# A graph layer on one core: node data fetched ahead of their blocks, edge rows stored in a new order, and SyncE's queue in program order

## The chip, the cores and the metric

The kernel runs on one core of a Trainium2 chip. The time is the device time of one execution, in microseconds (us); of before there are 14 runs with a median of 16,058.38 us (16,052.2 to 16,063.84). One more execution was profiled. Engines are called TensorE (PE, and PEld for its weight loads), VectorE (DVE), ScalarE (ACT), GpSimd (POOL) and SyncE (SP); SPq and so on are their instruction queues.

## The reference, cut to what matters

A graph has 50,000 nodes with 160 features each (64 scalars s, 32 vectors v of three parts) and 1,650,000 edges, sorted by their destination; 50,000 of them lead from a node to itself. Each edge has four numbers e (e0 and e1). A message is made for each edge and summed per destination:

```python
ss, vv = s[src], v[src]
dot = einsum('eui,ei->eu', vv, e1)
out0 = C0 * (ss * e0 @ W1 + dot * INV3 @ W2)
out1 = C1 * (p3 + p4 + p5)         # from ss, vv, e0, e1 and W3, W4, W5
m_agg = segment_sum(concat(out0, out1), dst)
h = concat(m_agg_s @ Ws, m_agg_v @ Wv)
y = x + relu(h);  out = layernorm(x + y)
```

A message is linear in x[src] and in e, so sums of e_k * x[src] over the edges of a node can be formed first, and one 640 x 160 weight matrix (BW, made of all seven W) applied to them.

## The kernel before, in words

**Plain and packed groups.** Edges are taken in groups of 6 x 128 (G = 6), two groups to a pair, twenty to a step `s` of the edge list. For each 128 edges GpSimd issues one indirect gather of 128 rows of x into the tile xg (L302), 12 to a pair. VectorE makes from the destinations a one-hot matrix of 32 slots (hot, L311) and multiplies it by the four numbers of each edge (ha, L314; three buffers). TensorE sums ha x xg into ps (L324), ScalarE copies it out (A, L327). xg has five buffers of a pair each (pool `rows`). The gather needs the index tile si, the matrix ha needs rel and pk; `place` (L262 to L296) makes all of them for one step s by transposes on TensorE.

**Self edges.** An edge from a node to itself needs no gather, since a block of nodes reads its own x in order anyway. So all but the first HEAD = 60 groups are packed beforehand: `pack(c)` reads 120 rows of 790 edges, finds in each row the self edges (`count`, `mark`, `collect`: their four numbers go to the tile mine), closes the holes that they leave by five shifts of 1, 2, 4, 8, 16 places (L490 to L506, two halves each), and stores the rows one after another into a list `edges` in DRAM, and mine into `selves`. There are 17 packs. Where a row begins in the list is known only at run time, from the table that `row_table` computes (L350); SyncE loads those numbers into registers (L519, L522) and issues two DMAs for each row, one to edges and one to selves (L540). Stored rows overlap by what the packing left over at their ends; so before, first all tails (from place 32 on), then all heads (32 places) are stored, in 12 rounds of up to 10 rows each. A later step s reads r from edges (L238).

**Blocks of 128 nodes.** Two pairs make a chunk: its sums are transposed (`turn`), multiplied by the weights (`apply_weights`) and kept (hp). Once the chunks of a block are complete, `nodes` loads xt (its x) and sa (its numbers from selves), `own` computes the block's own messages (ptx, xT, yx, t), `block` gathers the chunks' sums by a product (phb), adds t, and normalizes; `do_send` stores out.

**Order.** The main loop runs over the 1,043 pairs; `after_pair(p + n, f)` puts a piece of work n pairs later. The steps of a pack are spread evenly over the pairs up to a due pair, which lies one step s ahead of the first reader of the pack's rows. From this program order a scheduler makes the order on each engine, SyncE included. Every engine then works through its own list strictly in turn. SyncE issues nearly all plain DMAs: loads, row stores, sends.

**Start.** Before the loop the first step s is placed, the row table is made and the weights are multiplied together; SyncE also stores zeros into the first part of selves (L703).

Of the kernel before, what the change touches and what calls it, by code (L numbers as in the profile page):

```python
# [48 lines left out]
P = 128  # L49
# [18 lines left out]
HEAD = 60  # L68
# [31 lines left out]
def tile_gnn_resnorm(ctx: ExitStack, tc: tile.TileContext, x, src, dst, attr, W1, W2, W3, W4, W5, Ws, Wv, out, n_edges):  # L100
# [110 lines left out]
    with tc.tile_pool(name="once", bufs=1) as once, tc.tile_pool(name="raw", bufs=2) as rawp, \  # L211
            tc.tile_pool(name="idx", bufs=2) as idxp, tc.tile_pool(name="rows", bufs=5) as rowp, \
            tc.tile_pool(name="far", bufs=3) as farp, \
            tc.tile_pool(name="ops", bufs=3) as op, tc.tile_pool(name="sums", bufs=4) as sump, \
            tc.tile_pool(name="hp", bufs=alive + 4) as hpp, tc.tile_pool(name="node", bufs=3) as np_, \
            tc.tile_pool(name="psC", bufs=1, space=PSUM) as psC, tc.tile_pool(name="psK", bufs=2, space=PSUM) as psK, \
# [10 lines left out]
        dq = nc.sync  # L227
        offsets = {}
# [20 lines left out]
        def cast(loaded):  # L249
            s, n, ri, sf, df, af = loaded  # L250
            if ri is not None:
                rf = rawp.tile([P, 2, P], F32, name="rf")
                nc.scalar.copy(rf[:n], ri[:n])
                sf, df = rf[:n, 0, :], rf[:n, 1, :]
            if HELP:

                ro = rawp.tile([P, P], I32, name="ro")
                nc.scalar.mul(ro[:n], sf, 4.0 * D)
                offsets[s] = ro
            return s, n, sf, df, af  # L260

        def place(cast_):  # L262

            s, n, sf, df, af = cast_
            ng = n // G

            first = idxp.tile([P, SG], F32, name="first")
            nc.vector.tensor_scalar(first[:n], starts[:n], df[:, 0:1], None, op0=ALU.mult)
            nc.tensor.matmul(bank[:, 3, :ng], ones[:n], first[:n, :ng], start=True, stop=True)
            gs = slice(s * SG, s * SG + ng)  # L270
            nc.vector.tensor_scalar(baseB[:, gs], bank[:, 3, :ng], float(N - 1), None, op0=ALU.min)
            for g in range(QG):
                r = slice(g * W, (g + 1) * W)
                for c0, c1, h in ((s * SG // QG, (s * SG + ng) // QG, g),
                                  ((s * SG + ng) // QG, math.ceil((s * SG + ng) / QG), min(g, ng % QG - 1))):
                    if c0 < c1:
                        nc.vector.tensor_scalar(rowid[r, c0:c1],
                                                baseB[r, c0 * QG:c1 * QG].rearrange("p (c g) -> p c g", g=QG)[:, :, h],
                                                pidx[r], float(-g * W), op0=ALU.add, op1=ALU.add)
            pi = bank[:, 1:3, :]  # L280
            nc.tensor.transpose(pi[:, 0, :n], sf, ident[:n, :n])
            nc.tensor.transpose(pi[:, 1, :n], df, ident[:n, :n])
            pk = psK.tile([P, NK, P], F32, name="pk")
            for k in range(NK):
                nc.tensor.transpose(pk[:, k, :n], af[:, :, k], ident[:n, :n])
            si = idxp.tile([P, P], I32, name="si")
            nc.vector.tensor_scalar(si[:, :n], pi[:, 0, :n], 0.0, float(N - 1), op0=ALU.max, op1=ALU.min)
            rel = idxp.tile([P, P], F32, name="rel")

            nc.vector.scalar_tensor_tensor(  # L290
                rel[:, :n].rearrange("p (g j) -> p g j", j=G), pi[:, 1, :n].rearrange("p (g j) -> p g j", j=G),
                float(N - 1), baseB[:, gs].unsqueeze(2).to_broadcast([P, ng, G]),
                op0=ALU.min, op1=ALU.subtract)
            nc.vector.tensor_reduce(extremes[:, 0, s:s + 1], rel[:, :n], axis=AX.X, op=ALU.min)
            nc.vector.tensor_reduce(extremes[:, 1, s:s + 1], rel[:, :n], axis=AX.X, op=ALU.max)
            return si, rel, pk  # L296
# [53 lines left out]
        def row_table(tmp):  # L350

            NT = npacks * RP
            ti = once.tile([1, NT], I32, name="ti")
            at = tmp.tile([1, NT], F32, name="at")
            node = tmp.tile([1, NT], F32, name="node")
            nc.vector.memset(ti, 0)
            with nc.allow_non_contiguous_dma(reason="one number of each row"):
                dq.dma_start(ti[:, :NR], dst[EH:EH + NR * L].rearrange("(o r e) -> o r e", o=1, e=L)[:, :, 0])
            nc.gpsimd.iota(at, pattern=[[L, NT]], base=0, channel_multiplier=0, allow_small_or_imprecise_dtypes=True)
            most, least = math.ceil(EH / degree) + FAR, max(math.floor(EH / degree) - FAR, 0)  # L360
            nc.vector.tensor_scalar(node, ti, float(N), float(-most), op0=ALU.min, op1=ALU.add)
# [5 lines left out]
            nc.vector.tensor_copy(moved.bitcast(I32), node)  # L367
            nc.vector.tensor_copy(node, moved.bitcast(I32))
# [3 lines left out]
            nc.vector.tensor_scalar(moved, ti, float(N), None, op0=ALU.min)  # L372
            nc.vector.tensor_tensor(moved[:, :NR], moved[:, :NR], node[:, :NR], op=ALU.subtract)
            nc.vector.tensor_reduce(strayed[0:1, 0:1], moved[:, :NR], axis=AX.X, op=ALU.min)
            nc.vector.tensor_reduce(strayed[0:1, 1:2], moved[:, :NR], axis=AX.X, op=ALU.max)
            by_round = "o (c i j) -> o c j i"
            nc.vector.tensor_scalar(ti.rearrange("o (c j i) -> o c j i", c=npacks, j=RS),
                                    at.rearrange(by_round, c=npacks, j=RS), float(4 * C), None, op0=ALU.mult)
            nodes_at = moved.bitcast(I32)
            nc.vector.tensor_scalar(nodes_at.rearrange("o (c j i) -> o c j i", c=npacks, j=RS),  # L380
                                    node.rearrange(by_round, c=npacks, j=RS), float(4 * NK), None, op0=ALU.mult)
            return ti, nodes_at

        def pack(c):
# [128 lines left out]
            def store(head, j):  # L513

                m = len(range(j, n, RS))
                if not m:
                    return
                i0 = r0 + j * (RP // RS)
                _, at = nc.values_load_multi_w_load_instructions(  # L519
                    row_at[0:1, i0:i0 + m], engines=[ET.SP], min_val=0, max_val=row_start(NR - 1)[0][1] * 4 * C,  # L520
                    skip_runtime_bounds_check_because="held within bounds")
                _, node = nc.values_load_multi_w_load_instructions(  # L522
                    node_at[0:1, i0:i0 + m], engines=[ET.SP], min_val=0, max_val=row_start(NR - 1)[1][1] * 4 * NK,
                    skip_runtime_bounds_check_because="held within bounds")
                for i in range(m):
                    p = j + i * RS
                    (lo, hi), (nlo, nhi) = row_start(r0 + p)
                    v = nc.s_assert_within(at[i], lo * 4 * C, hi * 4 * C,
                                           skip_runtime_bounds_check_because="held within bounds")
                    e = slice(0, W) if head else slice(W, L)  # L530
                    put(edge_bytes, v, e, C, T["rows"][p:p + 1, e, :])
                    if r0 + p < real:
                        v = nc.s_assert_within(node[i], nlo * 4 * NK, nhi * 4 * NK,
                                               skip_runtime_bounds_check_because="held within bounds")
                        e = slice(0, W // 2) if head else slice(W // 2, W)
                        put(self_bytes, v, e, NK, T["mine"][p:p + 1, 0, e, :])

            def put(mem, at, e, width, what):
                size = (e.stop - e.start) * width * 4
                dq.dma_start(mem[e.start * width * 4:][ds(at, size)].rearrange("(o f) -> o f", o=1),  # L540
                             what.bitcast(U8).rearrange("p e c -> p (e c)"))
# [4 lines left out]
            for head in (False, True):  # L546
                steps += [partial(store, head, j) for j in range(RS)]
# [36 lines left out]
        def nodes(b):  # L584

            nb, row = rows_of(b)
            cs = of_block[b]
            xt = np_.tile([P, D], F32, name="xt")
# [3 lines left out]
            sa = np_.tile([P, NK], F32, name="sa")  # L592
            dq.dma_start(sa[:nb], selves[0, row.start * NK:row.stop * NK].rearrange("(n k) -> n k", k=NK))
            rr = np_.tile([P, alive], F32, name="rr")
# [4 lines left out]
            return xt, sa, hot2  # L599

        def own(b, xt, sa, hot2):
# [7 lines left out]
            t = np_.tile([P, D], F32, name="t")  # L609
# [12 lines left out]
            return xt, t, hot2  # L622
# [55 lines left out]
        placed = {0: place(cast(load(0)))}  # L678

        strayed = once.tile([P, 2], F32, name="strayed")  # L680
        nc.vector.memset(strayed, 0.0)
        moved = once.tile([1, npacks * RP], F32, name="moved")
        with tc.tile_pool(name="begin", bufs=1) as beginp:
            row_at, node_at = row_table(beginp)
            weights(beginp, psM)
        packp = later_pools.enter_context(tc.tile_pool(name="pack", bufs=1))
        limit = once.tile([P, 1], F32, name="limit")
        nc.vector.memset(limit, float(KM))
        place_ = once.tile([P, L], F32, name="place")
        nc.gpsimd.iota(place_, pattern=[[1, L]], base=0, channel_multiplier=0, allow_small_or_imprecise_dtypes=True)  # L690
        nc.vector.tensor_scalar(place_, place_, degree, None, op0=ALU.add)
# [6 lines left out]
        nc.vector.memset(counts[:, 1], float(W))  # L698

        nz = math.ceil((row_start(0)[1][1] + W) / P)  # L700
        zeros = once.tile([P, nz * NK], F32, name="zeros")
        nc.vector.memset(zeros, 0.0)
        dq.dma_start(selves[0, 0:P * nz * NK].rearrange("(p f) -> p f", p=P), zeros)  # L703
# [11 lines left out]
        def do_weights(c):  # L715
            hps[c] = apply_weights(*parts.pop(c))
            for b in after[c]:
                of_nodes[b] = nodes(b)
# [22 lines left out]

        raws, has = {}, {}
# [11 lines left out]
        done, began = 0, 0  # L754
        for p, (s, g, ng) in enumerate(pairs):
# [13 lines left out]
            if packs:  # L769
# [8 lines left out]
            if (g + ng) % QG == 0 or g + ng == NG:  # L778
                after_pair(p + 1, do_turn, c, sums)
                for b in after[c]:  # L780
                    after_pair(p + 3, do_own, b)
# [3 lines left out]
                    after_pair(p + 7, do_send, b)  # L785
# [197 lines left out]
```

## Time and profile before

| what | value |
|---|---|
| median of 14 runs | 16,058.38 us |
| the profiled execution's own time | 16,067.85 us |
| its span, first to last instruction | 16,066.1 us |
| GpSimd busy | 11,854.4 us (74%), 12,516 gathers |
| TensorE busy | 12,329.0 us (77%) |
| VectorE busy | 6,412.3 us (40%) |
| ScalarE busy | 1,573.8 us (10%) |
| granted TensorE clock, mean | 0.689 |
| moved by DMA | 1,218.18 MB, 76 GB/s |
| share of the chain that ended last | GpSimd 46%, issue 21%, TensorE 15%, DMA 13%, SyncE's queue 4% |
| first gather begins, last gather ends | 24.16 us, 16,012.55 us |

In a group's line stand the source line, engine and operation, what it writes and reads, and the count; then its busy time in all and the mean of one in ns; then the idle time of the engine just ahead of such instructions, and what ended most of it. "issue" is time in which an engine waited for nothing that the profile shows. In a list of waits each line names who waited for whom, the sum in us, how many times, and the longest. A timeline gives start and duration in us, and in brackets the idle time before. A table by stage gives for each stretch the busy time and count of PE, PEld, DVE, ACT and POOL, the granted clock, the DMA share and GB/s. A source line's row gives the shortest, median and longest duration in ns.

### The profile page before, as it was taken

How to read it: one execution, taken by the hardware profiler on the slowest of the kernel's cores; microseconds unless marked ns; L12 is line 12 of the kernel's file. 1: busy time of each engine (PE TensorE's matmuls, PEld its weight loads, DVE VectorE, ACT ScalarE, POOL GpSimd, SP SyncE). 2: the span in 40 equal slices, each digit the busy share in tenths (PEclk: the TensorE clock that was granted, in tenths of full speed). 3: DMA queues.
4: the chain of work that ended last, by engine and by line, in shares of the span. 5: the costliest groups of instructions: out<-in, count | busy, mean ns of one | idle time of the engine just before them, and what ended most of it. 6: DMA issues, size and time to landing. Idle time of an engine off the chain costs nothing.

```text
span 16066.1 us, 155475 instructions
## 1 busy us (share of the span) xinstructions
PE 12329.0 (77%) x47011; PEld 8690.3 (54%) x47012; DVE 6412.3 (40%) x15105; ACT 1573.8 (10%) x3873; POOL 11854.4 (74%) x12530
## 2 busy tenths in 40 slices
PE   6186877787778777787878777787878777787887
PEld 4155555555555555555555555555555555555555
DVE  4353434343443434353444434343444434253222
ACT  0011010010101010010101010010101010010100
POOL 7277777777777777777777777777777777777776
PEclk6576666666776767676776767676776666676666
DMA  2133333323333333333333333333333332332322
GB/s 72 34 76 79 77 81 76 81 73 82 75 80 77 78 80 77 80 76 80 75 81 77 78 78 77 80 76 78 75 81 77 78 78 74 77 76 76 75 72 62
DMA packets 813417, 1218.18 MB, mean 76 GB/s; under 512 B 288531, under 2 KB 591540, under 8 KB 808506
## 3 DMA queue, kind: packets, MB, share of 16 engines
q0 software_dynamic: 600768, 1026.11, 26.0%
q1 hardware_dynamic: 211196, 181.54, 4.2%
q8 instruction: 373, 6.11, 0.2%
q14 instruction: 472, 3.87, 0.1%
q10 hardware_dynamic: 608, 0.55, 0.0%
HBM read 1135.43 MB, written 71.86 MB: 75 GB/s over the span
## 4 chain that ended last, share of the span: by engine, by line
POOL 46%; issue 21%; PE 15%; DMA 13%; SPq 4%; DVE 1%; ACT 0%; POOLq 0%; DVEq 0%; ACTq 0%
POOL xg L302 46%; DMA xg<-in_x,si 12%; PE ps L324 7%; PE yx L614 2%; PE yx L613 2%; SPq L540 2%; PE pt L559 1%; PE phb L630 1%; PE phc L573 1%; SPq L522 1%; SPq L519 1%; PE ptx L607 0%; DMA edges<-prow 0%; DVE pra L465 0%; DVE prow L504 0%
## 5 line engine op out<-in xcount | busy, mean ns | idle before, releaser
L302 POOL DMA_INDIRECT xg<-in_x,si x12516 | 11850.1, 947 | 4157.6 <-issue 3573.0
L324 PE MATMUL ps<-xg,ha 128*128 128x160 f32 x25032 | 7379.0, 423 | 3190.3 <-DMA xg<-in_x,si 3133.5
L324 PEld LDWEIGHTS ps<-xg,ha 128*128 128x128 f32 x25032 | 4964.9, 253 | 5533.8 <-DMA xg<-in_x,si 4971.9
L314 DVE TENSOR_TENSOR ha<-hot,pk 128x1536 f32<-128x1536 f32 x1043 | 1825.5, 1750 | 5380.1 <-PE ps L324 5380.1
L465 DVE SCALAR_TENSOR_TENSOR pra<-marks,prow 120x236 bf16<-120x236 f32 (+40 forms) x2924 | 1499.2, 513 | 33.0
L327 ACT COPY A<-ps 128x320 f32<-128x320 f32 x1043 | 443.4, 425 | 6525.4 <-PE ps L324 6489.5
L614 PE MATMUL yx<-BWb,xT 32*128 32x320 f32 x1564 | 988.5, 727 | 0.9 <-ACT xT L608 0.9
L613 PE MATMUL yx<-BWa,xT 128*128 128x320 f32 x1564 | 954.3, 709 | 0.7 <-ACT xT L608 0.6
L559 PE MATMUL pt<-ident,A 128*128 128x128 f32 (+1 forms) x4172 | 916.9, 371 | 43.6 <-DVE t L620 31.0
L562 ACT COPY at<-pt 128x512 f32<-128x512 f32 (+1 forms) x1044 | 600.7, 580 | 3222.3 <-PE pt L559 3202.6
L630 PE MATMUL phb<-hp,hot 128*128 128x160 f32 x4688 | 897.3, 353 | 0.0
L630 PEld LDWEIGHTS phb<-hp,hot 128*128 128x128 f32 x4688 | 854.0, 237 | 15.8 <-ACT at L562 10.4
L573 PE MATMUL phc<-BWa,at 128*128 128x160 f32 x4176 | 783.2, 339 | 1.0 <-ACT at L562 1.0
L559 PEld LDWEIGHTS pt<-ident,A 128*128 128x128 f32 (+1 forms) x4172 | 642.8, 166 | 231.2 <-issue 113.1
L573 PE MATMUL phc<-BWb,at 32*128 32x160 f32 x4176 | 766.1, 326 | 0.0
L573 PEld LDWEIGHTS phc<-BWa,at 128*128 128x128 f32 x4176 | 727.3, 225 | 7.0 <-ACT at L562 6.4
L573 PEld LDWEIGHTS phc<-BWb,at 32*128 32x128 f32 x4176 | 632.6, 199 | 104.5 <-issue 104.5
L614 PEld LDWEIGHTS yx<-BWb,xT 32*128 32x128 f32 x1564 | 347.6, 276 | 601.0 <-ACT xT L608 299.0
L618 DVE TENSOR_SCALAR t<-yx,sa 128x160 f32<-128x160 f32 x391 | 149.3, 382 | 1194.4 <-PE yx L614 1193.3
L631 DVE TENSOR_TENSOR phb<-phb,t 128x160 f32<-128x160 f32 x391 | 129.6, 331 | 1184.3 <-PE phb L630 974.7
L620 DVE SCALAR_TENSOR_TENSOR t<-yx,sa,t 128x160 f32<-128x160 f32 x1173 | 443.2, 378 | 325.5 <-PE yx L614 319.8
L311 DVE TENSOR_TENSOR hot<-bank,rel 128x384 f32<-128x384 f32 x1043 | 562.0, 544 | 3.5
(148 smaller groups left out, 4539.2 us busy)
## 6 DMA issues: line engine op xcount, KB each, us to landing
xg<-in_x,si POOLq DMA_INDIRECT x12516
selves<-mine SPq DMA_DIRECT2D x4062, 0.2 KB
r<-edges SPq DMA_DIRECT2D x101, 360.0 KB
edges<-prow SPq DMA_DIRECT2D x2033, 17.8 KB
edges<-prow SPq DMA_DIRECT2D x2033, 0.8 KB
xt<-in_x SPq DMA_DIRECT2D x390, 80.0 KB
out<-o SPq DMA_DIRECT2D x390, 80.0 KB
pra<-in_attr SPq DMA_DIRECT2D x16, 1481.2 KB
```

Of the source, the lines that this page charges most:

```text
L302: nc.gpsimd.indirect_dma_start(out=xg[:, j, :], out_offset=None, in_=x, in_offset=bass.IndirectOffsetOnAxis(ap=placed[0][:, u + j:u + j + ...
L311: nc.vector.tensor_tensor(hot[:, :n], slotsP[:, 0:W].unsqueeze(1).to_broadcast([P, n, W]), rel[:, u:u + n].unsqueeze(2).to_broadcast([P, n ...
L314: nc.vector.tensor_tensor(ha[:, :n], hot[:, :n].unsqueeze(2).to_broadcast([P, n, NK, W]), pk[:, :, u:u + n].rearrange("p k u -> p u k").un ...
L324: nc.tensor.matmul(ps[:, j // G, :], ha[:, j].rearrange("p k w -> p (k w)"), xr, start=j % G == 0, stop=j % G == G - 1)
L327: evict(A[:, :ng], ps[:, :ng])
L465: nc.vector.scalar_tensor_tensor(T["waste"][:n, w0:w1], T["marks"][:n, w0 - a:w1 - a], float(w + 1), T["rows"][:n, w0:w1, 2 + k], op0=ALU. ...
L559: nc.tensor.transpose(pt[:f1 - f0, g, :], A[:, i, f0:f1], ident)
L562: evict(at[:, :, :ng].rearrange("f k g w -> f g k w"), pt[:f1 - f0, :ng].rearrange("f g (k w) -> f g k w", w=W))
L573: nc.tensor.matmul(ph[:ng * W], at[:, k, :ng].rearrange("f g w -> f (g w)"), bw[:, k, :], start=i == 0, stop=i == 2 * NK - 1)
L613: nc.tensor.matmul(y[:nb], xT[:, 0, :nb], BWa[:, ks, :], start=True, stop=False)
L614: nc.tensor.matmul(y[:nb], xT[:D - P, 1, :nb], BWb[:, ks, :], start=False, stop=True)
L630: nc.tensor.matmul(ph[:nb], hot2[:r, i, :nb], hp[:r], start=i == 0, stop=i == len(cs) - 1)
```

## The change

- HEAD goes from 60 to 100: the first 100 groups are plain, so they also gather their self edges.
- Rows are stored whole: first the rows of even number, then the odd ones, then the heads of the even ones again. The two tables of places become one (spots), read by one load of 20 numbers for each round; with offsets that begin at zero, a DMA needs no register operation. Each of the 18 rounds is followed by three empty steps.
- xt and sa are loaded by `ahead`, 7 pairs before the block's last pair, and own messages are made 3 pairs before it (7 buffers each for xt, sa, t); before, both came 2 to 3 pairs after. The send of out moves from 7 to 8 pairs after.
- SyncE keeps the program order (`manual_schedule`), the other engines are still scheduled.
- The weights and the row table (with the zeros) move from ahead of the loop to its first two pairs, behind the first step's cast, transposes and last reduction; packs begin at pair 2.
- xg has four buffers instead of five.

In the changed program there are 12,522 gathers and 1,044 ha; SyncE has 2,991 + 2,988 row DMAs (before 4,066 + 4,062), 306 register loads (816) and 3 register operations (4,066). On VectorE the ten half shifts of a pack stand nearly together, with at most two spreads (ha) among them; before, they lay among about 12.

```diff
-HEAD = 60
+HEAD = 100
...
-            tc.tile_pool(name="idx", bufs=2) as idxp, tc.tile_pool(name="rows", bufs=5) as rowp, \
+            tc.tile_pool(name="idx", bufs=2) as idxp, tc.tile_pool(name="rows", bufs=4) as rowp, \
...
+            tc.tile_pool(name="ahead", bufs=7) as aheadp, \
...
-                i0 = r0 + j * (RP // RS)
-                _, at = nc.values_load_multi_w_load_instructions(
-                    row_at[0:1, i0:i0 + m], engines=[ET.SP], min_val=0, max_val=row_start(NR - 1)[0][1] * 4 * C,
...
-                    node_at[0:1, i0:i0 + m], engines=[ET.SP], min_val=0, max_val=row_start(NR - 1)[1][1] * 4 * NK,
+                ni = RP // RS
+                i0 = (c * RS + j) * 2 * ni
+                _, spot = nc.values_load_multi_w_load_instructions(
+                    spots[0:1, i0:i0 + 2 * ni], engines=[ET.SP], min_val=0,
...
-                    e = slice(0, W) if head else slice(W, L)
-                    put(edge_bytes, v, e, C, T["rows"][p:p + 1, e, :])
+                    put(edge_bytes, v, T["rows"][p:p + 1, :W if head else L, :])
...
-            for head in (False, True):
-                steps += [partial(store, head, j) for j in range(RS)]
+            for head, j0 in ((False, 0), (False, 1), (True, 0)):
+                for j in range(j0, RS, 2):
+                    steps += [partial(store, head, j), None, None, None]
...
+        def ahead(b):
+
+            nb, row = rows_of(b)
+            xt = aheadp.tile([P, D], F32, name="xt")
+            dq.dma_start(xt[:nb], x[row, :])
...
+            sa = aheadp.tile([P, NK], F32, name="sa")
+            dq.dma_start(sa[:nb], selves[0, row.start * NK:row.stop * NK].rearrange("(n k) -> n k", k=NK))
+            return xt, sa
...
-            t = np_.tile([P, D], F32, name="t")
+            t = aheadp.tile([P, D], F32, name="t")
...
-        with tc.tile_pool(name="begin", bufs=1) as beginp:
-            row_at, node_at = row_table(beginp)
-            weights(beginp, psM)
...
+        START = 2
+        AHEAD = 7
...
+        for at, bs in zip(complete, after):
+            for b in bs:
+                after_pair(max(at - AHEAD, START - 1), do_ahead, b)
+                after_pair(max(at - AHEAD + 4, START), do_own, b)
+        later_pools.enter_context(tc.manual_schedule(engines={ET.SP}))
...
+            if p == START - 2:
+                with ExitStack() as behind, tc.tile_pool(name="begin", bufs=1) as beginp:
+                    for i in first_ones:
+                        behind.enter_context(tc.issue_after(i))
+                    weights(beginp, psM)
+            if p == START - 1:
+                with ExitStack() as behind, tc.tile_pool(name="table", bufs=1) as tablep:
+                    for i in first_ones:
+                        behind.enter_context(tc.issue_after(i))
+                    row_table(tablep)
...
-            if packs:
+            if packs and p >= START:
...
-                    after_pair(p + 3, do_own, b)
...
-                    after_pair(p + 7, do_send, b)
+                    after_pair(p + 8, do_send, b)
```

## Prediction, made before the changed kernel was run

> **What bounds the kernel now.** I read the page first. GpSimd issues one gather for each 128 edges, and its row is the largest that nothing else hides:
>
> ```profile
> L302 POOL DMA_INDIRECT xg<-in_x,si x12516 | 11850.1, 947 | 4157.6 <-issue 3573.0
> ```
>
> Each gather takes 947 ns and 0.30 us of issue follows it, so one starts every 1.251 us; 12,515 such steps make 15,652 us (by the finer 1.2507) of a span of 16,066.1. TensorE's 77% is an average that follows this beat: in the rest of the kernel it finishes a pair's sums 2.7 us after the pair's last gather. So the time is the gathers' beat, plus whatever stops GpSimd, plus the two ends. Next I asked what GpSimd waited for, and where:
>
> ```profile
> POOL xg L302 <- issue: 3573.0, 11726, 0.3
> POOL xg L302 <- DVE si L287: 306.0, 2, 286.2
> ...
> 485.80 0.95 POOL L302 DMA_INDIRECT xg<-in_x,si  x1 [0.30 <-issue]
> 772.90 0.94 POOL L302 DMA_INDIRECT xg<-in_x,si  x1 [286.16 <-DVE si L287]
> ```
>
> One hole of 286.2 us, and 19.9 us before the first gather. The chain of waits over 440 to 780 us says what fills the hole; the table by stage says that every engine is empty in it:
>
> ```profile
> by line: SPq L540 39.0%; issue 14.8%; SPq L519 12.7%; SPq L522 12.3%; DVE prow L504 7.9%; DVE pra L465 2.0%; DVE marks L497 1.7%; DVE pri L501 1.6%; DVE pri L502 1.4%; DVE pri L499 1.4%; DMA r<-edges 1.4%; DVE ha L314 0.5%; PE ps L324 0.3%;
> ...
> 762.43 4.59 DMA r<-edges
> ```
>
> ```profile
> 500.00:600.00 100.00, 0.00 (x0) 0.00 (x0) 0.00 (x0) 0.00 (x0) 0.00 (x0) 0.50 0.04 16
> 600.00:700.00 100.00, 0.00 (x0) 0.00 (x0) 0.00 (x0) 0.00 (x0) 0.00 (x0) 0.50 0.02 7
> ```
>
> SyncE is storing the first pack of rows, 480 DMAs from 493 to 761 us, and the first packed groups (r from edges) cannot be read before the last lands. VectorE had finished packing only at 494 us, GpSimd had used up its 60 plain groups (360 gathers) at 486 us. From SyncE's own rows: 12 rounds of tails take 143.4 us (0.392 us a DMA, with a register operation in it), 12 rounds of heads 124.6 us (0.322 us a DMA); the rest of a round is two register loads:
>
> ```profile
> L519 SPq TENSOR_LOAD <-ti x408: 956/1840/2700, 496.9 to 14890.4; - x136
> ```
>
> **The change, part by part, against the profiled execution (16,067.85 us, span 16,066.1).**
>
> *100 plain groups, shorter stores.* The first packed groups are wanted at gather 600, not 360. The first gather starts near 8.5 us (below) and the first pairs lose some 12 us, so gather 600 is due at 8.5 + 12 + 600 x 1.2507 = 771 us. Is the load there? In the changed order VectorE's last shift of the first pack stands behind 33 spreads (ha), and the 33rd needs the sums of pair 29, done near 470 us. The shifts then run almost without a break: ten of about 5.2 us (0.57 + 0.56 + 0.65 + 0.59 + 2.78 by the rows of L497 to L504), the last two 3.4 us, 48 us, so stores begin near 520 us. A pack is now 18 rounds (even rows whole, odd rows whole, even heads), 20 DMAs each, no register operation: 20 x 0.322 = 6.4 us, plus one load of 20 words. Two loads of 10 cost 3.6 us on the mean; the shortest single ones 1.2 us. The Trainium skill, "Runtime: NRT & Kernel Launch", Instruction fetch mechanics, speaks against a gain here: about 200 ns for each register even in bulk, so 20 words cost 4.0 us however they are split; the row (1,840 ns for 10) says 184 ns a word. I take 3.7 us: 10.1 us a round, 182 us a pack (158 with 2.4 us, 220 if a round stays at 12.2). With about 15 us for other DMAs on the queue the load is read at 722 us, and the index si, after casts and transposes, is ready near 735: 35 us early. TensorE's transposes of r stand after 46 pairs, near 710 us, so it waits about 15 us there, within its reserve. The hole goes: -285.9 us. At 220 us a pack it would leave under 10. The 100 groups carry self edges too: 12,522 gathers instead of 12,516, 6 x 1.25 = +7.5 us.
>
> *Start.* Now the first gather starts at 24.16 us: the ti load (14 us) stands ahead of what it needs on VectorE, and the zeros store takes 10.4 us on SyncE. With both behind, the first ra lands at 5.0 us, the second, issued right behind it, near 6.8. From the transposes to the gather took 4.1 us (20.02 to 24.16), 1.2 of them another step's. I take 8.5 us (8 to 12): -15.7. But the row table now runs beside gathers, and here a rule weighs:
>
> ```profile
> 24.10 2.26 DVE L364 SCALAR_TENSOR_TENSOR node<-at,node 1x2040 f32<-1x2040 f32 x1
> 24.16 3.83 POOL L302 DMA_INDIRECT xg<-in_x,si  x1 [19.88 <-DVE si L287]
> 26.67 1.20 DVE L365 TENSOR_SCALAR node<-node 1x2040 f32<-1x2040 f32 x1
> 27.93 1.20 DVE L367 CAST moved<-node 1x2040 int32<-1x2040 f32 x1
> 28.29 2.22 POOL L302 DMA_INDIRECT xg<-in_x,si  x1 [0.30 <-issue]
> 29.19 1.20 DVE L368 CAST node<-moved 1x2040 f32<-1x2040 int32 x1
> ```
>
> The first four gathers took 3.83, 2.22, 3.20, 2.69 us, 8.1 us over their beat, and two end 0.12 us after a table step ends. The skill's "SBUF — State Buffer" (SBUF: two separate sides) says that VectorE in its two-port mode, or with two SBUF inputs against a GpSimd operation that reads SBUF, shuts GpSimd out for the whole instruction. If it is cold code that slows the first gathers, nothing changes; by the rule 15 us of table steps now fall on gathers instead of 11.7, and at 8.1 / 11.7 they cost 10.5. I take +4 (0 to +7). The iota of the table goes into GpSimd's own queue after gather 43: 1.82 + 0.3 = +2.1. The weights (a chain of small products, stores and reloads) lie under the first pairs: wanted after 3.6 pairs (about 70 us), ready near 67; a few us late would be TensorE's alone.
>
> *x and own messages ahead; SyncE in program order.* At 1302 to 1470 us the second pack's stores hold up xt:
>
> ```profile
> PE ptx L607 <- DMA xt<-in_x: 72.8, 2, 50.6
> ...
> 1491.53 0.94 POOL L302 DMA_INDIRECT xg<-in_x,si  x1 [12.83 <-PE ptx L607]
> ```
>
> TensorE stands 50 us for x, falls 88 us behind, and the gathers lose 12.5 us. xt will be asked for 7 pairs before its block is complete and transposed 3 before: 4 pairs, 60 us of cover. -12.5 us. What is added: SyncE now waits in order, so a send of out (8 pairs after its block) holds xt, sa, r and stores behind it. A block's last product stands about 5 pairs after completion, so SyncE passes a send some 3 pairs (45 us) ahead of the gathers; TensorE waits for xt and r, GpSimd for si. Stores come at most 1.2 rounds a pair (72 of 279 steps over 60 pairs), 12 us plus 1 us of other DMAs out of 15, so no backlog grows. Without this cover, each us of delay is a us. Cost 0.
>
> *Row buffers 5 to 4.* TensorE may lag 3 pairs less the usual 2.7 us, 42 us, instead of 57. Outside the two places above its lag never passed 38.2 us. But the changed order bunches the shifts of every pack: 44 to 56 us of VectorE between two spreads. Spreads run up to three pairs (45 us) ahead, so TensorE gets 8 to 20 us behind: inside 42. Cost 0; if the cover failed, the surplus is paid in each of 17 packs.
>
> *Tail.* After the last sums TensorE now runs four blocks' own messages: 6.7 + 3.6 + 4.1 + 5.8 = 20.2 us of the 53.5 after the last gather. In the changed order none is left there. What is late next is the products of the last three blocks, which stay. -20.2 us.
>
> **Sum.** -285.9 - 15.7 - 12.5 - 20.2 + 7.5 + 4 + 2.1 = -320.7: span 15,745.4, own time 15,747. The profiled run lies 9.5 us above the median of before (16,058.38), so **15,738 us**, 2.0% less. Own range 15,705 to 15,770: the start, the table and the tail by 5 to 15 us each, and 13 us that slow gathers lost at 13.54 ms, which need not return.
>
> **Rivals.**
> 1. *Bunched shifts and four buffers.* If TensorE's lag passes 42 us by 10 in each of 16 packs, +160: 15,900. For: up to 56 us in which no spread or PSUM release comes, where before they were spread over 12 pairs. Against: the sum above leaves over 20 us. Chance 0.12.
> 2. *The hole only shrinks.* Stores begin at 540 and rounds cost 13 us: r near 795, and some 60 us stay: 15,800. For: VectorE finished 110 us after its position said (384 us) in before. Against: that was one run of steps which is now mostly spread. Chance 0.10.
> 3. *SyncE in order is slower than before.* To lose the 320 us, each of 16 packs must cost 20 us of gathers beyond about 90 us of reserve (SyncE's 45 us, the row buffers' 42): 110 us of backlog over 18 rounds, 6 us a round more than the 12 us a pair allows, so from about 18 us a round on. The longest round now is 12.2. A little beyond, 16,100. Chance 0.04.
>
> The first case has 0.74. A measurement of this kernel tells 0.2% (32 us) from no change. Faster by more (below 16,026): all of cases one and two of the rivals, bar 0.02, so 0.94; within 0.02; slower 0.04. The range runs from 15,700, where everything but the beat is at its best, to 15,860, which takes in the shrunken hole and half of rival 1.
>
> **What would show it.** Right: no gap over 20 us on GpSimd; r landing before 760 us; first gather by 12 us; rounds of 9 to 11 us; 30 to 36 us after the last gather. Wrong: GpSimd waiting for ps every 60 pairs (rival 1), for si near 771 us (rival 2), or TensorE waiting for xt or r in the middle (rival 3).

## The result, and the profile after

The changed kernel takes 15,824.84 us (median of 6 runs, 15,822.25 to 15,828.87) against 16,058.38 us: 0.9855 of the time before, 95% interval 0.9845 to 0.9864, so 1.45% less where 2.0% was forecast. The profiled execution took 15,823.29 us with a span of 15,821.5 us, 244.6 us less than before. The forecast for the span was 15,745.4 us: 76 us of the expected gain are missing.

What GpSimd waited for, in the changed kernel:

```profile
POOL xg L304 <- issue: 3597.3, 11809, 0.3
POOL xg L304 <- PE ps L326: 251.7, 547, 52.0
...
529.15 0.94 POOL L304 DMA_INDIRECT xg<-in_x,si  x1 [0.30 <-issue]
530.39 0.95 POOL L304 DMA_INDIRECT xg<-in_x,si  x1 [0.30 <-issue]
583.30 0.94 POOL L304 DMA_INDIRECT xg<-in_x,si  x1 [51.96 <-PE ps L326]
```

The wait of 286 us for si is gone. In its place stands one that the prediction did not have: 52 us for a free row buffer, that is, for TensorE's sums ps. A second of 27.7 us follows after the gather at 1,214.4 us. (Nearly all the rest of the 251.7 us is in waits of the length of the usual 0.3 us of issue.) Over the beat of 1.2507 us the two holes cost 51.7 and 27.4 us, 79.1 us in all: the size of the missing gain. What did TensorE wait for, and SyncE? Between 425 and 640 us:

```profile
PE ptx L616 <- DMA xt<-in_x: 95.9, 2, 91.7
...
SPq L543 <- DVE prow L510: 262.3, 1, 262.3
...
562.99 0.38 SPq L593 DMA_DIRECT2D xt<-in_x  x1
...
565.58 0.47 PE L616 MATMUL ptx<-ident,xt 128*128 128x128 f32 x1 [91.73 <-DMA xt<-in_x]
```

```profile
480.00:520.00 40.00, 0.00 (x0) 0.00 (x0) 38.23 (x90) 0.00 (x0) 30.25 (x33) 0.50 0.27 66
520.00:560.00 40.00, 0.00 (x0) 0.00 (x0) 18.66 (x15) 0.00 (x0) 8.60 (x10) 0.50 0.11 32
560.00:600.00 40.00, 33.31 (x174) 25.97 (x175) 11.82 (x25) 5.75 (x16) 12.74 (x14) 0.79 0.19 54
```

The two waits are to be read from the bottom up. SyncE keeps program order. It came to the first row store 262 us before VectorE had made the rows (the last shift ends at 539 us), and stood there. The load of xt for the block that TensorE handles after pair 29 stands behind that store and behind 24 us of further stores: it goes out at 563 us, and TensorE begins on it 2.6 us later. So TensorE stood 91.7 us (no matmul from 480 to 560 us in the table), used up its reserve of four row buffers, and GpSimd lost what was left over. The second hole is the same thing in the second pack: SyncE stands 224 us at the first store, TensorE waits 64.6 us for xt and GpSimd 27.7 us for ps.

The other lines that answer to those shown of before: SyncE's register loads, then the row table beside the gathers.

```profile
L526 SPq TENSOR_LOAD <-spots x306: 1379/1406/1766, 275.4 to 14898.3; - x153
```

```profile
79.49 2.26 DVE L371 SCALAR_TENSOR_TENSOR node<-at,node 1x2040 f32<-1x2040 f32 x1
79.79 3.51 POOL L304 DMA_INDIRECT xg<-in_x,si  x1 [0.30 <-issue]
81.97 1.20 DVE L372 TENSOR_SCALAR node<-node 1x2040 f32<-1x2040 f32 x1
```

A load of 20 words takes 1.4 us; two loads of 10 had taken 3.6 us on the mean. A gather that meets two steps of the table takes 3.51 us instead of 0.94 and ends 0.13 us after the second of them.

### The profile page after: what moved, and what is told of

It is laid out like the page before. It is cut to its first block, busy times and chain, and to the rows that moved or that the text cites. A ratio compares the mean times of both kernels' runs of the same rounds, so it can differ in the third digit from the quotient of the medians.

```text
span 15821.5 us, 146272 instructions
## 1 busy us (share of the span) xinstructions
PE 12177.9 (77%) x47031; PEld 8563.3 (54%) x47032; DVE 6392.4 (40%) x15106; ACT 1569.9 (10%) x3876; POOL 11851.4 (75%) x12536
## 4 chain that ended last, share of the span: by engine, by line
POOL 47%; issue 21%; PE 16%; DMA 12%; DVE 4%; ACT 0%; SPq 0%; ACTq 0%; DVEq 0%; POOLq 0%
POOL xg L304 47%; DMA xg<-in_x,si 11%; PE ps L326 7%; PE yx L623 3%; PE yx L622 2%; PE pt L564 2%; DVE prow L510 1%; PE phc L578 1%; PE phb L639 1%; DMA edges<-prow 1%; PE ptx L616 0%; DVE marks L503 0%; DVE pri L507 0%; DVE ha L316 0%; DMA r<-edges 0%
## 5 line engine op out<-in xcount | busy, mean ns | idle before, releaser
L326 PE MATMUL ps<-xg,ha 128*128 128x160 f32 x25044 | 6948.3, 411 | 2831.3 <-DMA xg<-in_x,si 2675.3
L326 PEld LDWEIGHTS ps<-xg,ha 128*128 128x128 f32 x25044 | 4812.2, 247 | 4888.1 <-DMA xg<-in_x,si 4369.1
L623 PE MATMUL yx<-BWb,xT 32*128 32x320 f32 x1564 | 1042.8, 764 | 0.0
L639 PE MATMUL phb<-hp,hot 128*128 128x160 f32 x4694 | 999.4, 379 | 8.7 <-ACT at L567 8.7
L622 PE MATMUL yx<-BWa,xT 128*128 128x320 f32 x1564 | 988.2, 732 | 5.5 <-ACT xT L617 5.5
L639 PEld LDWEIGHTS phb<-hp,hot 128*128 128x128 f32 x4694 | 933.2, 256 | 49.0 <-ACT at L567 45.8
L564 PEld LDWEIGHTS pt<-ident,A 128*128 128x128 f32 (+1 forms) x4174 | 602.5, 161 | 329.1 <-issue 228.0
L578 PEld LDWEIGHTS phc<-BWa,at 128*128 128x128 f32 x4176 | 714.8, 222 | 13.6 <-ACT at L567 12.5
L617 ACT COPY xT<-ptx 128x128 f32<-128x128 f32 (+2 forms) x782 | 204.0, 261 | 4511.0 <-PE ptx L616 4428.9
```

What stands on the lines that cost most here:

```text
L326: nc.tensor.matmul(ps[:, j // G, :], ha[:, j].rearrange("p k w -> p (k w)"), xr, start=j % G == 0, stop=j % G == G - 1)
L564: nc.tensor.transpose(pt[:f1 - f0, g, :], A[:, i, f0:f1], ident)
L578: nc.tensor.matmul(ph[:ng * W], at[:, k, :ng].rearrange("f g w -> f (g w)"), bw[:, k, :], start=i == 0, stop=i == 2 * NK - 1)
L622: nc.tensor.matmul(y[:nb], xT[:, 0, :nb], BWa[:, ks, :], start=True, stop=False)
L623: nc.tensor.matmul(y[:nb], xT[:D - P, 1, :nb], BWb[:, ks, :], start=False, stop=True)
L639: nc.tensor.matmul(ph[:nb], hot2[:r, i, :nb], hp[:r], start=i == 0, stop=i == len(cs) - 1)
```

## The experiments

One thing has to be known for the numbers. Of the twelve runs only one (shifts apart) fell on a chip like that of the first runs, where the kernel before takes 16,058 us. On the four chips of the other eleven (here the late chips) it takes 21,006 to 21,089 us. Their absolute times cannot be set beside the forecast; ratios to before on the same chip, and what waits for what, can be compared among themselves. I begin with what is different there.

**The changed kernel again.** No edit.

> The changed kernel once more, beside the kernel before on this call's chip. The first four experiments ran on a chip on which the kernel before takes 21,082 us instead of 16,058, and TensorE gets its instructions late. If this call's chip is like that of the first runs: 0.985 to 0.987 of before, about 15,825 us of 16,058. If it is the late one: TensorE is the bound, the 286 us of the hole weigh less there and four row buffers and bunched shifts weigh more; I expect 0.97 to 1.01 of before.

Measured: 20,358.71 us, 0.9692 of before (0.9674 to 0.9711), just under the range that was expected. A gather still takes 946 ns, but a pair takes 19.2 to 19.7 us in most stretches of 60 pairs instead of 15.04, and GpSimd waits 3,685 us for ps instead of 252. So GpSimd now waits for TensorE all along. Matmuls of one pair on it, from the timeline:

```profile
9015.07 1.90 PE L326 MATMUL ps<-xg,ha 128*128 128x160 f32 x12
9017.28 0.57 PE L326 MATMUL ps<-xg,ha 128*128 128x160 f32 x3 [0.31 <-issue]
9019.40 0.30 PE L326 MATMUL ps<-xg,ha 128*128 128x160 f32 x1 [1.56 <-issue]
9021.50 0.42 PE L326 MATMUL ps<-xg,ha 128*128 128x160 f32 x1 [1.81 <-issue]
```

Twelve matmuls follow one another at 0.14 us, then single ones 2 us apart, although the gathers that they read had ended 53 to 62 us earlier, and the last DMA packets of these gathers 1.2 to 1.6 us after that. "issue" means that the profile shows nothing awaited: 1,515 us of it stand ahead of ps, 31 us on the first chip. That TensorE gets its instructions late is my reading, and it cannot be all: TensorE also waits 1,801 us for ScalarE's xT (85 us on the first chip), and ScalarE and GpSimd stand some 10,300 and 912 us for something that the profile does not find on this core (none on the first chip). Two plain rivals fall short: the granted clock is 0.66 there against 0.69, under 4% less, and a DMA packet of the gathers takes 111 ns on the mean, on the first chip 112. The cause stays open. The first hole's chain is the same as on the first chip, only longer:

```profile
PE ptx L616 <- DMA xt<-in_x: 121.6, 1, 121.6
...
SPq L543 <- DVE prow L510: 304.9, 1, 304.9
```

**xt off SyncE.**

```diff
-            dq.dma_start(xt[:nb], x[row, :])
+            nc.scalar.dma_start(xt[:nb], x[row, :])
...
-            dq.dma_start(sa[:nb], selves
+            nc.scalar.dma_start(sa[:nb], selves
```

> The loads of xt and sa go out on ScalarE's queue, all else as in the changed kernel (15,825 us; two holes of 51.7 and 27.4 us over the beat on GpSimd, near 530 and 1,214 us). Theory 1: the holes come from SyncE, which stands 262 us in program order at the first row store and holds xt behind it; so both go, TensorE no longer waits for xt, and the time falls by 60 to 80 us, to about 15,750. Theory 1b: behind xt stand VectorE's bunched shifts of the first pack, which hold TensorE's PSUM buffers; then only the second hole goes and half of the first: about 15,775. Theory 2: the two first packs are squeezed into 37 and 49 pairs and four row buffers do not cover it, whatever xt does; both holes stay within 10 us, about 15,825.

> xt and sa on ScalarE's queue again, hoped to be on a chip like that of the first runs. There the changed kernel has holes of 51.7 and 27.4 us. On the late chip this kernel's TensorE no longer waited for xt, but 118 us for the first step of the next place (bank from first), which stands on VectorE behind the bunched shifts. Theory 1 (SyncE's hold of xt is the whole cause): both holes go, 15,745 us. Theory 1b (behind xt stand the shifts): the second hole goes, of the first 15 to 40 us stay: 15,765 to 15,790 us. If neither hole shrinks, 15,825 us, xt was not the cause.

Measured: 1.0305 of before (1.0286 to 1.0324) and 1.0307 (1.0285 to 1.0328), 6% slower than the changed kernel on such chips. Theory 1 falls in its simple form. Between 300 and 1,200 us TensorE no longer waits for xt, but (second run; the first gives 118.4 and 65.5 us):

```profile
PE bank L271 <- DVE first L270: 118.0, 1, 118.0
...
PE pk L287 <- DMA r<-edges: 63.5, 1, 63.5
```

The hole behind pair 36 stays, 134.8 and 129.5 us long. Behind the late xt stands `first`, the first step of the next `place`, which VectorE has after the bunched shifts; behind that stands r, since the stores come late too (SyncE stands 392 us at the first). Over the whole run TensorE waits 2,192 us for r (63 times) instead of 699 us (15 times), which goes with the 6%; why r is late there so often stays open.

**SyncE scheduled.**

```diff
-        later_pools.enter_context(tc.manual_schedule(engines={ET.SP}))
```

> Only SyncE's program order is undone: its queue is arranged by the scheduler, as before the change. Theory 1 (the order holds xt, and issues a pack's four reads in one burst, which costs the gathers 1.5 to 2.5 us a pack): the holes shrink to under 20 us in all and the bursts cost less; 15,730 to 15,770 us. Rival: the program order is what keeps stores and reads early enough, and without it GpSimd waits for r or si as in the kernel before: over 15,850 us.

> SyncE scheduled, 100 groups, again. On the late chip TensorE did not wait for xt in the first packs, but 107 us for the first packed groups (r), since the scheduler set loads and sends between the stores. On a chip like that of the first runs the groups are wanted earlier in time, at 771 us: I expect a hole of 30 to 90 us near pair 46, and back the 79 us of the two others and 15 to 25 us of the bursts: 15,750 to 15,815 us. If SyncE's program order is what removed the old hole of 286 us, over 15,900 us.

Measured: 0.9128 (0.9109 to 0.9146) and 0.9126 (0.911 to 0.9142): with the program order undone the kernel is 6% faster than the changed kernel on these chips. TensorE waits in the first packs neither for xt nor for `first`, but for r, and there GpSimd's hole is now (107.7 and 105.2 us):

```profile
PE pk L287 <- DMA r<-edges: 105.1, 1, 105.1
```

Why r is late here is not what the second expectation says. One store goes out at 702 us; the other 359 begin at 789 us, when VectorE's last shift ends, and take 207 us. In the changed kernel on such a chip the 360 stores take 277 us, but begin at 681 us. So the stores are shorter and VectorE is later. The first pack's hole is as long either way (100 us in the changed kernel there), only earlier and for xt. What differs over the whole run is SyncE: it stands 8 us in all for the rows of a store (prow), against 3,765 us, and TensorE waits once for r, against 15 times (699 us). But in this kernel the ten half shifts of a pack also lie among 3 to 6 spreads instead of 0 to 2: VectorE's order, too, was made differently because SyncE's was. Which of the two gives the 6% was to be told by the next kernel but one.

**SyncE scheduled, 140 plain groups.** As the last, with

```diff
-HEAD = 100
+HEAD = 140
```

> The changed kernel with SyncE's queue arranged by the scheduler and 140 plain groups instead of 100. With SyncE scheduled alone, the hole came back as a wait of TensorE for the first packed groups (r, 107 us), while xt and the shifts of the packs no longer held it. 40 more groups are 20 pairs, 308 us of beat: r then lies in time, and no hole of over 20 us is left; 8 more gathers cost about 10 us. On a chip like that of the first runs: about 15,740 us (15,720 to 15,765), 0.980 of before, under the changed kernel by 70 us or more. On a chip where TensorE's instructions come late: about 100 us below the 19,257 us with SyncE scheduled alone, 0.906 to 0.911 of before. Rival: what holds TensorE in the first packs is the squeezed pack work on VectorE, not SyncE's order; then a hole of over 25 us stays near pair 36.

> SyncE scheduled and 140 groups, again. On the late chip it left no hole over 26 us. On a chip like that of the first runs: 15,825 less 79 (the two holes) less 15 to 25 (the bursts of reads) plus 7.5 us (6 more gathers): 15,735 us (15,720 to 15,760), the fastest of all. If a hole of over 25 us stays, above 15,770.

Measured: 0.907 (0.9055 to 0.9085) and 0.9063 (0.9046 to 0.908), as expected for such a chip by the first text. No wait of TensorE for xt, `first` or r is left between 300 and 1,200 us, and GpSimd's longest for ps is 26 us. So on these chips the first pack's hole has three layers, one behind the other: xt, `first` behind the shifts, r. Taking away one shows the next; with room for all three it is gone.

**Shifts apart.** SyncE stays in program order; each half shift is put behind the latest spread, with three empty steps after it.

```diff
+            def behind_spread(g):
+                with tc.issue_after(spreads[-1]):
+                    next(g, None)
...
-                steps += [partial(next, g, None)] * (4 if 2 << b <= KM else 2)
+                steps += [partial(behind_spread, g), None, None, None] * (4 if 2 << b <= KM else 2)
```

> The changed kernel with SyncE still in program order, but the shifts of a pack held apart: each half shift stands behind the latest spread (ha), with three empty steps after it, so they lie among 4 spreads instead of 0 or 1, and no stretch of VectorE without a spread is over about 30 us (before 44 to 56). Theory: of the 1,100 us by which SyncE's scheduled queue (19,257 us) beat the changed kernel (20,359 us, the same kind of chip, on which TensorE has no reserve), most came by VectorE's order, because the planner bunches the shifts when SyncE keeps program order; then this kernel gains 300 us or more, 0.945 to 0.955 of before. Rival: it came from SyncE's queue itself (xt, r and reads late behind stores); then within 100 us of the changed kernel, 0.965 to 0.973. On a chip like that of the first runs, where TensorE's reserve covers the bunches, both say within 15 us of 15,825 us.

Measured, on a chip like the first (before 16,057.52 us): 15,765.41 us (15,764.97 to 15,769.22), 0.9819 of before (0.9803 to 0.9836), 59 us less than the changed kernel and the fastest version measured on such a chip. I had expected under 15 us: a miss, and a useful one. The gain is in the holes: the second is gone, and the first has shrunk:

```profile
592.04 0.95 POOL L305 DMA_INDIRECT xg<-in_x,si  x1 [0.30 <-issue]
615.94 0.94 POOL L305 DMA_INDIRECT xg<-in_x,si  x1 [22.95 <-PE ps L328]
```

```profile
PE ptx L622 <- DMA xt<-in_x: 59.5, 1, 59.5
...
SPq L549 <- DVE prow L512: 218.9, 1, 218.9
```

What I had overlooked: the empty steps also move the first store later in program order. In SyncE's list 10 loads of xt stand ahead of it instead of 8. The xt that is held is that of a later block, and it is held 59.5 us instead of 91.7. The hole follows the wait: 91.7 us of waiting gave a hole of 51.7, 64.6 gave 27.4, 59.5 gave 22.7, and a wait of 22.3 us, later among this kernel's first stores, gave none. In its second pack TensorE does not wait for xt, though SyncE stands 147.3 us at the first store there: what stands behind it is not wanted yet. Each hole is the wait for xt less 37 to 40 us, which is what the four row buffers cover. Both edits act in this kernel; how much of it the shifts gave, and how much the later store, it does not tell. In the other packs SyncE now stands 82 to 109 us at the first store instead of 190 to 218, the wait of TensorE for r that the changed kernel has there (see below) is gone, and TensorE's largest lag fell from 36 to 39 us to 17 to 27 us, which cost no time here in either kernel. What the same kernel does where TensorE has no reserve was not seen, so what gives the scheduled queue its 6% there stays open.

**60 plain groups.**

```diff
-HEAD = 100
+HEAD = 60
```

> Only HEAD goes back from 100 to 60, so the first packed group is wanted at gather 360, near 470 us. If the 100 groups are what removes the hole of 286 us, it returns: shifts end near 480 us at the earliest, 18 rounds of 9.3 us take 167 us, index and transposes about 30 us more, so si is ready near 680 us and GpSimd waits about 200 us; with 6 gathers less, about 16,000 us (15,950 to 16,040). If the new order of stores and of SyncE were enough by itself, under 15,900 us.

Measured: 20,465.66 us, 0.9708 (0.969 to 0.9727), no clear difference from the changed kernel's 0.9692 (0.9674 to 0.9711). Expected was a wait for si of about 200 us; there is none over 7 us. Instead SyncE stands 369 us at the first store, TensorE waits four times for xt between 300 and 1,200 us, 288.9 us in all, and GpSimd for ps, 134.9, 49.5 and 25.1 us before gather 360 and 37.4 us ahead of it. These holes hide the rows rather than acquit them: si for the first packed groups is ready only at 766.7 us, 26 us after the last plain gather ended. Without the holes GpSimd would have been there some 200 us earlier (an estimate: their sum). So this run does not show that 60 groups are enough; it shows that at 60 groups xt is late first.

**Before, with 100 plain groups alone.** Same edit, in the other direction, on the kernel before.

> The kernel before with HEAD = 100 and nothing else of the change. If the 100 groups carry nearly all of the gain: stores begin near 540 us, the old 24 rounds take 268 us, si is ready near 825 us against gather 600 due at 787 us, so a hole of about 40 us stays of 286, and 6 gathers add 7.5 us: about 15,820 us (15,800 to 15,870), as fast as the whole change. If the shorter stores and the order of SyncE are needed as well, the hole keeps over 100 us: above 15,900 us.

> The kernel before with 100 groups alone, again. Old stores: 268 us from about 540 us, si ready near 825 us against gather 600 due near 787 us: a hole of about 40 us instead of 286, and 7.5 us for 6 gathers: 15,820 us (15,800 to 15,870), 0.983 to 0.988 of before. If shorter rounds are needed as well, over 15,900 us.

Measured: 0.9836 (0.9817 to 0.9855) and 0.986 (0.984 to 0.988). The ratio came as expected, not the way to it: a wait for si of 199 and 202 us stays, where 40 us were expected. One store goes out at 663 us, but the rest begin only at 771 us, when VectorE's last shifts end, and take 342 us for the old 24 rounds. In the changed kernel on such a chip the 18 rounds begin at 681 us and take 277 us, and there is no wait for si. So on these chips the shorter stores and an earlier start of them were needed for that hole. And in the second run TensorE waits 2,679 us for xt, 55 times, against 223 us, twice, in the changed kernel: the loads made ahead work, outside the first two packs.

**Reads spread.** Each pack's large read is cut in four, with empty steps between.

```diff
-            steps += [read, None, None, None, begin]
+            steps += [read] + [s for a in range(0, RP, 30) for s in (None, partial(read_part, a, a + 30))] + [None, begin]
```

> The changed kernel, but each pack's four reads (2.2 MB) no longer go out within 1.7 us: the large one (pra) is cut into four parts, each a step of its own with an empty step between, some 5 us apart and more. The theory of a burst: in the recorded trace of the changed kernel the gathers that follow such a burst lose 1.5 to 2.5 us a pack, about 25 us in all, which the kernel before did not lose; spread out, most of it comes back: 15,800 to 15,812 us where the changed kernel takes 15,825, on the chip of the first runs, or about 0.1% less than the changed kernel on this call's chip. Rival: the loss is one of bytes (the same DMA engines carry them, whenever they come), then within 5 us of the changed kernel.

Measured: 0.9679 (0.9656 to 0.9702) beside 0.9692 (0.9674 to 0.9711) for the changed kernel on the same chip. The intervals overlap, and where GpSimd waits for TensorE all along a slower gather can cost nothing. Nor does the edit change the reads alone: TensorE no longer waits for r (699 us before), but 839 us for xt, 19 times instead of twice. This settles nothing. The theory of the burst stands on the first chip's traces (below).

## Why the prediction was right and wrong

The time lies in the range that was given (15,700 to 15,860 us), but not in its own narrower one (15,705 to 15,770), and the upper end was drawn for rivals 1 and 2, neither of which came as told. That a hole of another origin ended inside it is luck. The sum, term by term, on the two profiled executions (the rest is what the terms leave):

| step | forecast, us | measured, us |
|---|---|---|
| hole for si | -285.9 | -285.9 |
| 6 more gathers | +7.5 | +7.5 |
| start (first gather 24.16 to 9.30) | -15.7 | -14.9 |
| row table and iota beside gathers | +6.1 | +0.3 |
| xt ahead, the hole at 1,491 us | -12.5 | -12.5 |
| SyncE in program order | 0 | +79.1 |
| four row buffers | 0 | 0 |
| tail (53.5 to 28.6 after the last gather) | -20.2 | -24.9 |
| rest | | +6.7 |
| span | -320.7 | -244.6 |

**The hole: right.** Stores begin at 539 us (forecast 520), the 18 rounds take 170 us from then (182), and the first packed gather, at 825.7 us after the new hole, waits for nothing; its index si is ready at 783.5 us. TensorE's transposes for it, at 781 us, do not wait for r, which was asked for at 712.6 us. Without the new hole they would stand near 730 us (781 less 51.7, an estimate), still behind r. A round takes 9.4 us instead of 10.1, other DMAs of the queue included, since the load of 20 words takes 1.4 us, not 3.7. The term was over-sized by the mean of before's row; its shortest loads of 10 words, near 1.2 us, were nearer. The Trainium skill, "Runtime: NRT & Kernel Launch" (Instruction fetch mechanics), has about 200 ns a register for loads from HBM, from which I weighed an estimate of 4.0 us against it; here, from a tile in SBUF, it is 70 ns a word. Rival 2 asked for stores at 540 us and rounds of 13 us: half of it came.

**SyncE in program order: wrong.** This is the step that failed: "4 pairs, 60 us of cover" for xt and "SyncE passes a send some 3 pairs (45 us) ahead of the gathers", at "Cost 0". I looked for the late thing among sends and counted rounds a pair. The late thing was the first row store itself, which waits for VectorE. Its place in program order lies so far ahead of VectorE that SyncE stands at it in every pack, and what stands behind it is late over all cover. Over the whole run:

```profile
SPq L543 <- DVE prow L510: 3544.6, 17, 262.3
...
PE pk L287 <- DMA r<-edges: 486.2, 15, 34.1
PE ptx L616 <- DMA xt<-in_x: 160.5, 3, 91.7
```

In the first two packs, squeezed into 37 and 49 pairs, SyncE stands 262 and 224 us and xt is late by 91.7 and 64.6 us. In the other fifteen it stands 190 to 218 us and r is late by 31 to 34 us. For example, in the third pack the first store goes out at 2,018.5 us, and then:

```profile
2027.76 0.37 SPq L240 DMA_DIRECT2D r<-edges  x1
...
2032.36 0.49 PE L287 MATMUL pk<-ident,r 120*128 120x120 f32 x1 [34.11 <-DMA r<-edges]
```

I had the two pieces in hand: the shifts end some 50 us after 470 us, and SyncE runs in order. I did not ask what else stands behind the first store. Rival 3 named the sign (TensorE waiting for xt or r) and all packs, but another mechanism, a backlog of stores, and 20 us each. The wait came in all 17 packs; it cost time in two, 51.7 and 27.4 us, and was covered in the rest. The experiment with shifts apart agrees with this in size, the one with xt off SyncE shows its limit: on the late chips xt, freed alone, gives way to the next late thing. With only xt freed on a chip like the first, nothing was measured.

**Four row buffers: right, with less room than said.** I expected the bunched shifts to set TensorE back 8 to 20 us. Counted from the end of a pair's last gather to the end of its last product, usually 2.6 us, TensorE's lag reaches 36 to 39 us in every pack after the first two (in the kernel before 26 us at most outside the two places, not the 38.2 of the prediction). What sets it back is mainly the wait for r, 31 to 34 us, not the shifts. On the same count the three holes (96.7, 72.5 and, with shifts apart, 67.7 us of lag; 51.7, 27.4 and 22.7 us lost) all put the reserve at 45 us. So 6 us were left, and rival 1 missed by that, though for another reason than it gave.

**Start and row table.** The start came within 1 us. The table costs the gathers nearly nothing more than before: the first pairs lose 12.4 us, before 12.1, although its steps now fall on other gathers. The very first gather now takes 1.10 us instead of 3.83, and the slow ones stand beside the table, so it was not cold code. The Trainium skill's "SBUF — State Buffer" (SBUF: two separate sides) fits the single gathers (3.51 us, released when the steps end), but the sum that I built on it, +4, was too high (15 x 8.1 / 11.7 less the 8.1 lost before gives 2.3); with the iota it was to be 6.1 and is 0.3.

**The tail** was under-sized by 4.7 us.

**The rest**, +6.7 us, is made of parts that the traces show, against each other. Gathers that start over 0.1 us late cost 33.8 us after 2,000 us, before 21.8, of which 13.0 lay in one place at 13.54 ms that did not come back: +12.0. Two bursts of reads before 2,000 us (below) add 4.0. The step of all other gathers is 0.8 ns shorter (1,250.05 against 1,250.81 ns), -9.3. What is new stands at 13 of the 14 packs read after 2,000 us: SyncE in program order issues the four reads of a pack, often r too, within 2 us, and 10 to 15 us later GpSimd loses 1.5 to 3.2 us:

```profile
3216.20 0.43 SPq L401 DMA_DIRECT2D pri<-in_src  x1
3216.68 0.41 SPq L402 DMA_DIRECT2D pri<-in_dst  x1
3217.13 0.40 SPq L404 DMA_DIRECT2D pri<-in_dst  x1
3217.57 0.41 SPq L405 DMA_DIRECT2D pra<-in_attr  x1
3218.08 0.35 SPq L240 DMA_DIRECT2D r<-edges  x1
...
3227.49 0.94 POOL L304 DMA_INDIRECT xg<-in_x,si  x1 [0.30 <-issue]
3230.82 0.94 POOL L304 DMA_INDIRECT xg<-in_x,si  x1 [2.38 <-PE ps L326]
```

The kernel before had the same in small, which I overlooked: its large read went out alone, and in 12 of the 13 packs read after 2,000 us one gather 10 to 12 us later was 0.3 to 1.5 us late. For one of them:

```profile
11727.74 0.35 SPq L399 DMA_DIRECT2D pra<-in_attr  x1
...
11739.04 0.95 POOL L302 DMA_INDIRECT xg<-in_x,si  x1 [1.76 <-DMA xg<-in_x,si]
```

The DMA packets in both traces say that the reads do it: the last packet of a gather (48 packets each, taken in order) ends 1.3 us after it as a rule, and after the first 200 us it ends over 5 us after it only within 11 us of a large read's issue (110 gathers, up to 9.5 us; before 61, up to 7.9 us). How much the bunching by itself adds is not shown.

**Not settled.** What part of the 59 us the spacing of the shifts gave, and what the later store; whether the scheduled queue, best on the late chips, is also best on a chip like the first; what gives it the 6% there; and why those chips are late.

## What to carry to other kernels

Where a queue is put in program order, go through every instruction on it that waits for an engine, ask how early the queue reaches it, and list what stands behind it: the loads behind one store that waited 262 us cost more than any send. A wait that costs nothing may still be there, as r was in fifteen packs, 6 us inside the reserve. Steps that are spread evenly up to a due date are squeezed in the first rounds; sum the first rounds by themselves. A hole has layers: before calling one wait its cause, find what is late next, as xt, then `first`, then r here.

## What was not expected of the hardware

The same program took 15,825 us on one chip and 20,359 us on another, and the kernel before 16,058 and 21,006 us: 29% and 31% longer, with gathers of the same 946 ns and matmuls that stand some 2 us apart with nothing awaited. What a change is worth moved with it: the changed kernel 0.9855 there, 0.9692 here. A register load of 20 words takes 1.4 us, where two of 10 took 3.6 us. While a pack's large read goes out on SyncE's queue, the gathers' rows land up to 7.4 to 9.5 us after the gather instead of 1.3 us.
